# Gathering the rows of the conditional expert tiles ahead, and one last stage behind both programs

## The chip, the cores and the metric

The kernel runs on one core of one Trainium2 chip. The metric is the device time of one execution in microseconds (us), the median of several runs. A profile is one execution recorded by the hardware; its span reaches from the first instruction to the last.

## What is computed

The reference is two layers on an image of 256 channels and 48 x 48 pixels, that is 2304 tokens of 256 numbers:

```
x = x + conv_attention(group_norm(x))          # 9216 x 9216 scores, softmax without a maximum
t = tokens(x)
t = t + slice_attention(layer_norm(t))
t = t + ffn(layer_norm(t))                     # 8 experts, each token goes to 2 of them
x = image(t)
# ffn, for every token: the two largest of 8 gate values, softmax over the two, then
#   out += weight * (gelu(t @ W1[e] + b1[e]) @ W2[e] + b2[e])      for its two experts e
```

## The kernel before

The whole kernel is one function, `layers`, which the program holds twice. The first program computes the attention sums without subtracting a maximum. While it runs it notes the largest and smallest of these sums, and makes a verdict of one number, `bad`. The wrapper `tile_conv_attn_hybrid_kernel` loads `bad` into a register of every engine (L1170) and enters a second program under a branch (`tc.If(again > 0)`, L1173), which does everything again with maxima. With these inputs `bad` is 0 and the second program is jumped over.

The change touches the expert stage and what follows it. The router has put the 4608 (token, expert) pairs into tiles of 128 rows, each of one expert. At least `SURE` = 36 tiles are always used; up to `NSL` = 43 can be. `slot_t` holds the token numbers of each tile, `slot_w` the weights, `expert_i` each tile's expert, and `used_i` how many tiles are used. For a tile s:

- `load(s)` (L1030) gathers the 128 token rows from the DRAM tensor `tn_d` into a buffer `xs`, by an indirect DMA that GpSimd (POOL) issues (L1033), and loads the expert's first matrix, 1 MB, into `w1` by a DMA of SyncE (SP, L1040). Both have rings of two buffers.
- `turn` transposes the rows on TensorE (PE): two matmuls `pt`, copied by VectorE (DVE) to `xT`.
- `first` does 32 matmuls `ph` (first matrix) and eight Gelu activations on ScalarE (ACT).
- `second` does 16 matmuls `py` (second matrix, which lies in SBUF for all experts). After six of them it calls `meanwhile`, which turns the rows of a coming tile. Then DVE adds the bias and multiplies by the weight into `y`, and POOL adds the 128 rows of `y` to the DRAM tensor `t_d` with an indirect DMA (L1090). Each such addition waits for the one before it to land.

The sure tiles run in a plain loop with two tiles in flight: `first(s)`, the loads of tile s+2, then `second(s-1)`. The tiles from 36 on stand in nested branches (L1132 to L1136), since their number is known only at run time:

```
for s in range(SURE, NSL):
    more.enter_context(tc.If(used > s))
    if s + 1 < NSL:
        loaded[s + 1] = load(s + 1)
    second(s, first(s, *turned.pop(s)), lambda: turn_next(s + 1))
```

So inside the body of tile s the rows of tile s+1 are gathered, and `second(s)` turns them. Three of these bodies are entered in the profiled execution: tiles 36, 37 and 38.

The last stage stands at the end of `layers`: five DMAs of SP read `t_d` into tiles `tt`, PE transposes them (L1155), DVE and ACT copy them to `ob` (L1159, L1161), and SP writes five blocks of the output. Each of the two programs has its own copy of this stage.

Order: calls through `pe`, `dve`, `act`, `pool` and `sp` are pinned to the order of the program on their engine (the helper at L57, which is why most rows of the profile bear L57). Calls through `nc.gpsimd` and `nc.sync`, such as the gathers, the additions to `t_d` and the `w1` loads, are placed by the framework's scheduler, which also inserts all semaphores. The content of a branch is placed as a unit. Where a branch is not entered, every engine passes a short block that raises its semaphores to what the skipped code would have left; on POOL this block holds one INC_SWDGE_SEM for the semaphores of the DMAs that POOL issues.

Of the kernel before, what the change touches and what calls it, by code (L numbers as in the profile page):

```python
# [9 lines left out]
FP = mybir.dt.float32  # L10
# [5 lines left out]
P = 128  # L16
C = 256
NT = 2304
# [18 lines left out]
NSL = (2 * NT - E) // P + E  # L37
SURE = 2 * NT // P
# [24 lines left out]
def layers(  # L63
    ctx: ExitStack,
    tc: tile.TileContext,
    bad,
    x, Wq, bq, Wk, bk, Wv, bv, Wo, bo,
    W0, b0, Ws, bs, Wqkv, bqkv, Wout, bout,
    Wg, bg, W1, b1, W2, b2,
    out,  # L70
):

    nc = tc.nc
    x_v = x[0].rearrange("(c p) h w -> p c (h w)", p=P)
    out_v = out[0].rearrange("(c p) h w -> p c (h w)", p=P)

    const = ctx.enter_context(tc.tile_pool(name="const", bufs=1))
    pe, dve, act, pool, sp = (  # L80
        InOrder(tc, e) for e in (nc.tensor, nc.vector, nc.scalar, nc.gpsimd, nc.sync)
    )
    small = ctx.enter_context(tc.tile_pool(name="small", bufs=2))


    ident = const.tile([P, P], FP, name="ident")
    make_identity(nc, ident)
    ones = const.tile([P, P], FP, name="ones")
    nc.vector.memset(ones, 1.0)

# [3 lines left out]
        out=gmat, in_=gmat, pattern=[[-8, 16], [0, 8]], compare_op=ALU.is_ge,  # L94
# [3 lines left out]
        out=gmat, in_=gmat, pattern=[[8, 16], [0, 8]], compare_op=ALU.is_ge,  # L98
# [24 lines left out]
    )  # L123
    dram = ctx.enter_context(tc.tile_pool(name="dram", bufs=1, space=bass.MemoryType.DRAM))
    tn_d = dram.tile([NT + P, C], FP, name="tn_d")
    t_d = dram.tile([NT + P, C], FP, name="t_d")
    empty = const.tile([P, C], FP, name="empty")
    nc.vector.memset(empty, 0.0)
    token1 = const.tile([P, NTT], FP, name="token1")
# [107 lines left out]
    with proj, tc.tile_pool(name="ps_pj", bufs=5, space=PSUM) as ps_pj, tc.tile_pool(  # L237
        name="ps_w", bufs=2, space=PSUM
# [175 lines left out]
    def turn(i, ps):  # L414

        for c in range(2):
            pe.transpose(ps[:, C + c * P : C + (c + 1) * P], tn[:, i % 6, c * P : (c + 1) * P], ident)

        def keep():
            act.copy(tnT[:, i % 3], ps[:, C : 2 * C].rearrange("p (c t) -> p c t", c=2))  # L420

        return [(4, keep)]
# [592 lines left out]
    with tc.tile_pool(name="ps_h", bufs=1, space=PSUM) as ps_h, tc.tile_pool(  # L1015
        name="ps_y", bufs=1, space=PSUM
    ) as ps_y, tc.tile_pool(name="ps_t", bufs=1, space=PSUM) as ps_t, tc.tile_pool(
        name="ps_j", bufs=1, space=PSUM
    ) as ps_j:

        def ring(pool, n, shape, name):
            return cycle([pool.tile(shape, FP, name=f"{name}{k}") for k in range(n)])

        ring_xs, ring_w1 = ring(fp, 2, [P, C], "xs"), ring(fp, 2, [P, 2, HID], "w1")
        ring_xT, ring_hid = ring(fp, 2, [P, 2, P], "xT"), ring(fp, 2, [P, NHC, P], "hid")
        ring_y = ring(fp, 2, [P, C], "y")
        ring_ph, ring_py = ring(ps_h, 3, [P, 4, P], "ph"), ring(ps_y, 2, [P, C], "py")
        ring_pt = ring(ps_t, 2, [P, 2, P], "pt")

        def load(s):  # L1030

            xs = next(ring_xs)
            nc.gpsimd.indirect_dma_start(  # L1033
                out=xs, out_offset=None, in_=tn_d[:, :],
                in_offset=bass.IndirectOffsetOnAxis(ap=slot_t[:, s : s + 1], axis=0),
                bounds_check=NT + P - 1, oob_is_err=True,
            )
            w1 = next(ring_w1)
            e = expert_of(s, mybir.EngineType.SP)
            nc.sync.dma_start(  # L1040
                out=w1, in_=W1[bass.ds(e, 1)].rearrange("e (c p) f -> p (e c) f", p=P)
            )
            return xs, w1

        def turn(xs):

            pt = next(ring_pt)
            for c in range(2):
                pe.transpose(pt[:, c, :], xs[:, c * P : (c + 1) * P], ident)
            xT = next(ring_xT)  # L1050
            dve.tensor_copy(xT, pt)
            return xT

        def first(s, xT, w1):

            e = expert_of(s, mybir.EngineType.Activation)
            hid = next(ring_hid)
            for f0 in range(0, NHC, 4):
                ph = next(ring_ph)
                for f in range(f0, f0 + 4):  # L1060
                    for c in range(2):
                        pe.matmul(
                            ph[:, f - f0, :], w1[:, c, f * P : (f + 1) * P], xT[:, c, :],
                            start=(c == 0), stop=(c == 1),
                        )
                for f in range(f0, f0 + 4):
                    act.activation(
                        hid[:, f, :], ph[:, f - f0, :], AF.Gelu, bias=b1_e[:, bass.ds(e, 1), f],
                    )
            return hid  # L1070

        def second(s, hid, meanwhile):

            e = expert_of(s, mybir.EngineType.PE)
            py = next(ring_py)
            for f in range(NHC):
                pe.matmul(
                    py, hid[:, f, :],
                    w2_sb[:, bass.ds(e, 1), f, :].rearrange("p e d -> p (e d)"),
                    start=(f == 0), stop=(f == NHC - 1),  # L1080
                )
                if f == 2:
                    meanwhile()
            e = expert_of(s, mybir.EngineType.DVE)
            y = next(ring_y)
            dve.tensor_tensor(
                y, py, b2_e[:, bass.ds(e, 1), :].rearrange("p e d -> p (e d)"), ALU.add
            )
            dve.tensor_scalar(y, y, slot_w[:, s : s + 1], None, ALU.mult)
            nc.gpsimd.indirect_dma_start(  # L1090
                out=t_d[:, :], out_offset=bass.IndirectOffsetOnAxis(ap=slot_t[:, s : s + 1], axis=0),
                in_=y, in_offset=None, bounds_check=NT + P - 1, oob_is_err=True,
                compute_op=ALU.add,
            )

        loaded = {s: load(s) for s in range(2)}
        turned, hid = {}, {}

        def turn_next(s):
            if s < NSL:  # L1100
                xs, w1 = loaded.pop(s)
                turned[s] = turn(xs), w1

        def judge():

            both = fp.tile([P, 2], FP, name="both", tag="judge")
            for k, op in enumerate((ALU.max, ALU.min)):
                dve.tensor_reduce(both[:, k : k + 1], ends_of[:, k, :], AX.X, op)
            dve.tensor_scalar(both[:, 0:1], both[:, 0:1], HIGH, None, ALU.is_gt)
            dve.tensor_scalar(both[:, 1:2], both[:, 1:2], LOW, None, ALU.is_lt)  # L1110
            dve.tensor_tensor(both[:, 0:1], both[:, 0:1], both[:, 1:2], ALU.max)
            pm = ps_j.tile([1, P], FP, name="pm")
            pe.transpose(pm, both[:, 0:1], ident)
            dve.tensor_reduce(bad, pm, AX.X, ALU.max)

        turn_next(0)
        for s in range(SURE):
            hid[s] = first(s, *turned.pop(s))
            if s + 2 <= SURE:
                loaded[s + 2] = load(s + 2)  # L1120
            if s == 0:
                turn_next(1)
            else:
                second(s - 1, hid.pop(s - 1), lambda: turn_next(s + 1))
            if s == 4 and bad is not None:
                judge()
        second(SURE - 1, hid.pop(SURE - 1), lambda: None)
        used = nc.values_load(
            used_i, min_val=0, max_val=NSL,
            skip_runtime_bounds_check_because="it is a sum of counts, cut at NSL",  # L1130
        )
        with ExitStack() as more:  # L1132
            for s in range(SURE, NSL):
                more.enter_context(tc.If(used > s))
                if s + 1 < NSL:
                    loaded[s + 1] = load(s + 1)  # L1136
                second(s, first(s, *turned.pop(s)), lambda: turn_next(s + 1))


    with tc.tile_pool(name="fin", bufs=len(TBLOCKS)) as fin, tc.tile_pool(  # L1140
        name="ps_f", bufs=4, space=PSUM
    ) as ps_f:
# [7 lines left out]
        for (t0, n), tt in zip(TBLOCKS, tts):  # L1150
# [9 lines left out]
                else:  # L1160
                    nc.scalar.copy(ob[:, c, 0:n], pt[:, 0:n])  # L1161
            sp.dma_start(out=out_v[:, :, t0 : t0 + n], in_=ob[:, :, 0:n])


@with_exitstack
def kernel(ctx: ExitStack, tc: tile.TileContext, *args):
    verdict = ctx.enter_context(tc.tile_pool(name="verdict", bufs=1))
    bad = verdict.tile([1, 1], mybir.dt.int32, name="bad")
    layers(tc, bad, *args)
    again = tc.nc.values_load(  # L1170
        bad, min_val=0, max_val=1, skip_runtime_bounds_check_because="it is the result of a comparison"
    )
    with tc.If(again > 0):  # L1173
        layers(tc, None, *args)


# [33 lines left out]
```

## Time and profile before

| | us |
|---|---|
| median of 3 runs | 1649.94 (1649.25 to 1652.01) |
| the profiled execution's own time | 1650.91 |
| its span, first to last instruction | 1649.2 |
| PE busy in the span | 1576.2 (96%) |
| DVE, ACT, POOL busy | 1046.9, 810.0, 147.1 |
| start to the end of the router, by stretch | 0 to 1324 |
| sure tiles | about 1324 to 1592 |
| conditional tiles | about 1592 to 1626 |
| last stage, jump over the second program, end | about 1626 to 1649.2 |

In the timelines each line has the start, the duration, the engine, line and operation, the tile written and those read, the count, and in square brackets how long the engine had been idle and what ended that. "PEld" is PE's weight load. A "q" behind an engine's name means its sequencer, which waits, loads registers, branches and issues DMAs without being busy. In the views of one line, the durations are the smallest, the median and the largest in ns, and then come the first and the last start in us.

### The profile page before, as it was taken

The page shows a single profiled execution, that of the slowest core. Times are in us where ns is not written, and L with a number is a line of the kernel's source. Part 1 is how long each engine was busy: PE and PEld are TensorE (multiplying, and loading weights), DVE is VectorE, ACT ScalarE, POOL GpSimd, SP SyncE. Part 2 cuts the span into 40 slices and gives each one's busy share as a digit, 9 for nine tenths or more (in the row PEclk, how much of TensorE's full clock was granted, in tenths as well). Part 3 has the DMA queues.
Part 4 walks back from the last instruction along what each step waited for, and adds up shares of the span by engine and source line. Part 5 has one row for each costly group of instructions (what it writes and reads, how often), then busy time and mean ns, then how long its engine had stood idle before and what let it go on. Part 6 is the DMA issues. An engine that isn't in the chain of part 4 may idle for free.

```text
span 1649.2 us, 31729 instructions
## 1 busy us (share of the span) xinstructions
PE 1576.2 (96%) x13178; PEld 795.1 (48%) x13178; DVE 1046.9 (63%) x1361; ACT 810.0 (49%) x1100; POOL 147.1 (9%) x126
## 2 busy tenths in 40 slices
PE   7999999999999999999999999999997589999984
PEld 3633443333333333333333333333345489999984
DVE  6577777687777786886877877868774811111111
ACT  2355555565655655655655556556551323333321
POOL 0000000000000000000000000000000323333321
PEclk9999999999999999999999999999996689999998
DMA  4000000000000000000000000000006356666655
GB/s 134 1 1 1 1 1 1 1 1 1 2 1 1 2 1 2 1 1 1 1 1 1 1 1 1 1 1 1 1 2 230 115 183 187 173 185 191 174 143 160
DMA packets 39735, 78.87 MB, mean 48 GB/s; under 512 B 3534, under 2 KB 26139, under 8 KB 39451
## 3 DMA queue, kind: packets, MB, share of 16 engines
q1 hardware_dynamic: 32042, 66.35, 11.9%
q0 software_dynamic: 7536, 10.36, 3.6%
q8 instruction: 108, 1.77, 0.5%
q14 instruction: 49, 0.39, 0.1%
HBM read 64.24 MB, written 12.45 MB: 47 GB/s over the span
## 4 chain that ended last, share of the span: by engine, by line
PE 92%; DVE 3%; DMA 2%; issue 2%; ACT 0%; POOL 0%; SPq 0%; ACTq 0%; POOLq 0%; DVEq 0%
PE s L57 33%; PE av L57 33%; PE ph L57 8%; PE py L57 8%; PE pa L57 2%; PE pb L57 1%; PE pw L57 1%; PE pp L292 1%; PE pp L296 1%; PE pp L321 1%; DMA t_d<-y,slot_t 1%; PE pt L57 1%; DMA Wq_raw<-in_L_conv_Wq_dram 0%; DVE s L57 0%; PE pm L57 0%
## 5 line engine op out<-in xcount | busy, mean ns | idle before, releaser
L57 DVE TENSOR_TENSOR acc<-acc,p 128x1024 f32<-128x1024 f32 x612 | 748.0, 1222 | 256.8 <-ACT p L57 248.6
L57 ACT ACTIVATE p<-s 128x1024 f32<-128x1024 f32 x648 | 662.7, 1023 | 493.5 <-PE s L57 483.4
L57 PE MATMUL av<-p,v_sb 64*64 64x512 f32 x5184 | 675.8, 590 | 1.4 <-ACT p L57 0.7
L57 PE MATMUL s<-q,kk 64*64 64x512 f32 x5184 | 674.9, 589 | 0.0
L57 PEld LDWEIGHTS s<-q,kk 64*64 64x64 f32 x5184 | 202.0, 133 | 351.2 <-issue 180.9
L57 PEld LDWEIGHTS av<-p,v_sb 64*64 64x64 f32 x5184 | 195.9, 131 | 358.0 <-ACT p L57 202.3
L57 ACT ACTIVATE hid<-ph,bcol 128x128 f32<-128x128 f32 x312 | 89.0, 368 | 231.2 <-PE ph L57 217.6
L57 PEld LDWEIGHTS ph<-xT,w 128*128 128x128 f32 x1248 | 148.0, 195 | 3.0 <-DVE xT L57 0.9
L57 PE MATMUL py<-w_sb,hid 128*128 x624 | 149.3, 383 | 0.0
L57 PE MATMUL ph<-xT,w 128*128 128x128 f32 x1248 | 148.3, 278 | 0.5 <-DVE xT L57 0.5
L57 POOL TENSOR_TENSOR rstd_t<-ve,mhalf 128x1 f32<-128x1 f32 (+1 forms) x21 | 27.6, 1313 | 1251.0 <-DVE ve L57 1251.0
L57 DVE COPY xT<-pt 128x256 f32<-128x256 f32 x40 | 17.0, 424 | 181.2 <-PE pt L57 181.2
L57 PEld LDWEIGHTS py<-w_sb,hid 128*128 128x128 f32 x624 | 114.2, 193 | 12.7
L1090 POOL DMA_INDIRECT t_d<-y,slot_t x39 | 61.8, 1585 | 101.5 <-DVE y L57 91.2
L57 DVE TENSOR_TENSOR y<-py,b_bc 128x256 f32<-128x256 f32 x39 | 16.5, 424 | 70.7 <-PE py L57 70.7
L1033 POOL DMA_INDIRECT xs<-tn_d,slot_t x40 | 42.6, 1066 | 105.7 <-PE pt L57 96.2
L57 DVE RECIPROCAL rinv<-pb 128x256 f32<-128x256 f32 x18 | 31.5, 1749 | 0.0
L57 PE MATMUL pt<-ident,xs 128*128 128x128 f32 x80 | 16.2, 283 | 11.8 <-DMA xs<-tn_d,slot_t 11.8
L57 DVE TENSOR_TENSOR acc<-p 128x1024 f32<-128x1024 f32 x18 | 22.1, 1225 | 8.4 <-ACT p L57 8.4
L309 DVE TENSOR_SCALAR q<-pp,bcol 64x512 f32<-64x512 f32 (+1 forms) x30 | 20.8, 694 | 8.8 <-PE pp L292 8.4
L57 PE MATMUL pw<-what,t_sb 128*128 128x86 f32 x72 | 15.7, 422 | 6.7 <-POOL what L57 6.7
L57 DVE TENSOR_REDUCE up<-av 128x512 f32<-128x1024 f32 x18 | 21.9, 1216 | 0.0
(248 smaller groups left out, 601.9 us busy)
## 6 DMA issues: line engine op xcount, KB each, us to landing
w<-in_L_ffn_W_dram SPq DMA_DIRECT2D x40, 1024.0 KB
w_sb<-in_L_ffn_W_dram SPq DMA_DIRECT2D x8, 1024.0 KB
x_sb<-in_x_dram SPq DMA_DIRECT2D x4, 576.0 KB
t_d<-t_sb SPq DMA_DIRECT2D x3, 768.0 KB
tn_d<-tn SPq DMA_DIRECT2D x3, 768.0 KB
tt<-t_d SPq DMA_DIRECT2D x4, 512.0 KB
out_dram<-ob SPq DMA_DIRECT2D x4, 512.0 KB
b_bc<-in_L_ffn_b_dram SPq DMA_DIRECT2D x1, 1024.0 KB
```

Of the source, the lines that this page charges most:

```text
L57: return self.tc.keep_in_program_order(getattr(self.engine, name)(*args, **kwargs))
L292: nc.tensor.matmul(pq[:, 0:tn], WqT[:, c, cols], xn[:, c, toks], start=(c == 0), stop=(c == 1))
L296: nc.tensor.matmul(pk[:, 0:tn], WkT[:, c, cols], xn[:, c, toks], start=(c == 0), stop=(c == 1))
L309: nc.vector.tensor_scalar(dst, pq[rows, 0:tn], bcol[rows, B_Q + m : B_Q + m + 1], 0.125, ALU.add, ALU.mult,)
L321: nc.tensor.matmul(pv[:, 0:C], xn[:, c, i * P : (i + 1) * P], WvT[:, c, :], start=(c == 0), stop=(c == 1),)
L1033: nc.gpsimd.indirect_dma_start(out=xs, out_offset=None, in_=tn_d[:, :], in_offset=bass.IndirectOffsetOnAxis(ap=slot_t[:, s : s + 1], axis= ...
L1090: nc.gpsimd.indirect_dma_start(out=t_d[:, :], out_offset=bass.IndirectOffsetOnAxis(ap=slot_t[:, s : s + 1], axis=0), in_=y, in_offset=None ...
```

## The change

The gathers of the tiles 36 to 42 are moved out of the branches into the loop of the sure tiles, with a buffer of their own for each (seven tiles `late_xs` of 128 x 256). They are written into the iterations s = 17 to 23. `load` is split into `rows` (gather) and `load_w1`. The `w1` loads stay where they are. In all, 43 gathers are then issued where the profiled execution issued 40.

The last stage is taken out of `layers` and put behind the branch of the second program, where both programs share it; `t_d` and the identity `ident`, which it uses, are made by the wrapper. So the register load of `bad` and the jump over the second program now stand ahead of the last stage; before, they stood behind it.

```diff
@@ layers, expert stage
+        late_xs = iter([fp.tile([P, C], FP, name=f"late_xs{s}") for s in range(SURE, NSL)])
-        def load(s):
-            xs = next(ring_xs)
+        def rows(s, xs):
             nc.gpsimd.indirect_dma_start(out=xs, ...)
+            return xs
+
+        def load_w1(s):
             w1 = next(ring_w1)
...
-        loaded = {s: load(s) for s in range(2)}
+        for s in range(2):
+            xs[s], w1[s] = rows(s, next(ring_xs)), load_w1(s)
...
         for s in range(SURE):
-            hid[s] = first(s, *turned.pop(s))
+            hid[s] = first(s, xT.pop(s), w1.pop(s))
+            if s + 2 < SURE:
+                xs[s + 2] = rows(s + 2, next(ring_xs))
             if s + 2 <= SURE:
-                loaded[s + 2] = load(s + 2)
+                w1[s + 2] = load_w1(s + 2)
+            ahead = s + 1 - SURE // 2
+            if 0 <= ahead < NSL - SURE:
+                xs[SURE + ahead] = rows(SURE + ahead, next(late_xs))
...
                 more.enter_context(tc.If(used > s))
                 if s + 1 < NSL:
-                    loaded[s + 1] = load(s + 1)
-                second(s, first(s, *turned.pop(s)), lambda: turn_next(s + 1))
+                    w1[s + 1] = load_w1(s + 1)
+                second(s, first(s, xT.pop(s), w1.pop(s)), lambda: turn_next(s + 1))
@@ wrapper
+    make_identity(nc, ident)
+    t_d = dram.tile([NT + P, C], FP, name="t_d")
-    layers(tc, bad, *args)
+    layers(tc, bad, ident, t_d, *args[:-1])
     again = nc.values_load(bad, ...)
     with tc.If(again > 0):
-        layers(tc, None, *args)
+        layers(tc, None, ident, t_d, *args[:-1])
+    sp = InOrder(tc, nc.sync)
+    with tc.tile_pool(name="fin", ...) as fin, ...:     # the last stage, moved here as it was
...
```

More of the change, by code (lines that the diff above doesn't have):

```diff
@@ L65, in layers @@
     tc: tile.TileContext,
-    bad,
+    bad, ident, t_d,
     x, Wq, bq, Wk, bk, Wv, bv, Wo, bo,
@@ L69, in layers @@
     Wg, bg, W1, b1, W2, b2,
-    out,
 ):
@@ L76, in layers @@
     x_v = x[0].rearrange("(c p) h w -> p c (h w)", p=P)
-    out_v = out[0].rearrange("(c p) h w -> p c (h w)", p=P)
     const = ctx.enter_context(tc.tile_pool(name="const", bufs=1))
-    pe, dve, act, pool, sp = (
-        InOrder(tc, e) for e in (nc.tensor, nc.vector, nc.scalar, nc.gpsimd, nc.sync)
-    )
+    pe, dve, act, pool = (InOrder(tc, e) for e in (nc.tensor, nc.vector, nc.scalar, nc.gpsimd))
     small = ctx.enter_context(tc.tile_pool(name="small", bufs=2))
-    ident = const.tile([P, P], FP, name="ident")
-    make_identity(nc, ident)
     ones = const.tile([P, P], FP, name="ones")
@@ L125, in layers @@
     tn_d = dram.tile([NT + P, C], FP, name="tn_d")
-    t_d = dram.tile([NT + P, C], FP, name="t_d")
     empty = const.tile([P, C], FP, name="empty")
@@ L1042, in load @@
             )
-            return xs, w1
+            return w1
         def turn(xs):
@@ L1094, in second @@
             )
-        loaded = {s: load(s) for s in range(2)}
-        turned, hid = {}, {}
+        xs, w1, xT, hid = {}, {}, {}, {}
+        for s in range(2):
+            xs[s], w1[s] = rows(s, next(ring_xs)), load_w1(s)
         def turn_next(s):
             if s < NSL:
-                xs, w1 = loaded.pop(s)
-                turned[s] = turn(xs), w1
+                xT[s] = turn(xs.pop(s))
         def judge():
@@ L1135, in layers, with kernel @@
                 if s + 1 < NSL:
-                    loaded[s + 1] = load(s + 1)
-                second(s, first(s, *turned.pop(s)), lambda: turn_next(s + 1))
+                    w1[s + 1] = load_w1(s + 1)
+                second(s, first(s, xT.pop(s), w1.pop(s)), lambda: turn_next(s + 1))
+@with_exitstack
+def kernel(ctx: ExitStack, tc: tile.TileContext, *args):
+    nc = tc.nc
+    out_v = args[-1][0].rearrange("(c p) h w -> p c (h w)", p=P)
+    both = ctx.enter_context(tc.tile_pool(name="both", bufs=1))
+    bad = both.tile([1, 1], mybir.dt.int32, name="bad")
+    ident = both.tile([P, P], FP, name="ident")
+    make_identity(nc, ident)
+    dram = ctx.enter_context(tc.tile_pool(name="t", bufs=1, space=bass.MemoryType.DRAM))
+    t_d = dram.tile([NT + P, C], FP, name="t_d")
+    layers(tc, bad, ident, t_d, *args[:-1])
+    again = nc.values_load(
+        bad, min_val=0, max_val=1, skip_runtime_bounds_check_because="it is the result of a comparison"
+    )
+    with tc.If(again > 0):
+        layers(tc, None, ident, t_d, *args[:-1])
+    sp = InOrder(tc, nc.sync)
     with tc.tile_pool(name="fin", bufs=len(TBLOCKS)) as fin, tc.tile_pool(
@@ L1162, in layers @@
             sp.dma_start(out=out_v[:, :, t0 : t0 + n], in_=ob[:, :, 0:n])
[L1165 to L1168, printed above, removed]
-    layers(tc, bad, *args)
[L1170 to L1173, printed above, removed]
-        layers(tc, None, *args)
 _INS = [
```

## The prediction

> **What bounds the kernel now.** I read the page first: PE is busy 96% of the span and carries 92% of the chain that ended last. A change that doesn't touch PE's work can gain only where PE stands idle, so I looked for idle PE in the two stretches that the change touches. The windows by stage give 263.8 us of PE work in the 268 us of the sure tiles, 25.6 in the 34 us of the conditional tiles, and 5.9 in the last 24 us. The timeline of PE from 1587 us on shows the holes:
>
> ```profile
> 1592.57 3.73 PE L57 MATMUL ph<-xT,w 128*128 128x128 f32 x32
> 1596.14 1.46 PE L57 MATMUL py<-w_sb,hid 128*128 x6
> 1601.87 0.69 PE L57 MATMUL pt<-ident,xs 128*128 128x128 f32 x2 [4.27 <-DMA xs<-tn_d,slot_t]
> 1602.35 4.47 PE L57 MATMUL py<-w_sb,hid 128*128 x10
> 1606.62 3.91 PE L57 MATMUL ph<-xT,w 128*128 128x128 f32 x32
> 1610.36 1.46 PE L57 MATMUL py<-w_sb,hid 128*128 x6
> 1614.21 0.44 PE L57 MATMUL pt<-ident,xs 128*128 128x128 f32 x2 [2.39 <-DMA xs<-tn_d,slot_t]
> ...
> 1622.66 0.44 PE L57 MATMUL pt<-ident,xs 128*128 128x128 f32 x2 [0.98 <-DMA xs<-tn_d,slot_t]
> 1622.93 2.32 PE L57 MATMUL py<-w_sb,hid 128*128 x10
> 1634.55 4.36 PE L1155 MATMUL pt<-ident,tt 128*128 128x128 f32 x24 [9.29 <-DMA tt<-t_d]
> ```
>
> In each conditional body the transposes of the next rows wait for the gather, and the ten `py` behind the longest wait take 4.47 us, where the same ten take 2.32 in the third body. The timeline of POOL says why the gather is late: it is issued in the body, right behind the addition of the tile before.
>
> ```profile
> 1594.89 1.55 POOL L1090 DMA_INDIRECT t_d<-y,slot_t  x1 [2.94 <-PE ph L57]
> 1596.75 1.10 POOL L1033 DMA_INDIRECT xs<-tn_d,slot_t  x1 [0.30 <-issue]
> 1607.96 1.58 POOL L1090 DMA_INDIRECT t_d<-y,slot_t  x1 [10.11 <-DVE y L57]
> ...
> 1626.39 1.58 POOL L1090 DMA_INDIRECT t_d<-y,slot_t  x1 [5.46 <-DVEq L1132]
> ```
>
> Behind the last addition comes the last stage. The chain that ended last has this addition's landing, the first `tt` load and the transposes in a row. Meanwhile POOL goes to the end of the branches (L1132), loads `bad` (L1170), and jumps over the second program (L1173). The views of these lines give its steps:
>
> ```profile
> 1626.39 3.84 DMA t_d<-y,slot_t
> 1630.38 4.04 DMA tt<-t_d
> ...
> L1132 POOLq INC_SWDGE_SEM  x1: 1775/1775/1775, 1626.9 to 1626.9; - x1
> ...
> L1170 POOLq TENSOR_LOAD <-bad x1: 311/311/311, 1628.9 to 1628.9; - x1
> ...
> L1173 POOLq EVENT_SEMAPHORE  x6: 17/30/43, 1632.0 to 1632.4; - x6
> L1173 POOLq COMPARE_BRANCH  x1: 55/55/55, 1629.3 to 1629.3; - x1
> L1173 POOLq INC_SWDGE_SEM  x1: 1746/1746/1746, 1632.5 to 1632.5; - x1
> L1173 PEldq COMPARE_BRANCH  x1: 4167/4167/4167, 1641.1 to 1641.1; - x1
> ```
>
> The reader is to see two things here: POOL is through with the jump only at 1634.3, 7.9 us behind the issue of its last addition; and nobody waits for that now, for the `tt` loads start at 1630.4.
>
> **The change part by part.**
>
> *Gathers out of the branches: minus 10.8 us.* In the sure loop a tile costs PE 3.57 (`ph`) + 1.30 (six `py`) + 0.22 (`pt`) + 2.16 (ten `py`) = 7.25 us, start to start; POOL's additions repeat at just that distance. Three bodies at this pace end at 1592.57 + 21.75 = 1614.3. They end now at about 1625.1 (1622.93 + 2.16). So 10.8 us: 7.6 of it is the waiting itself, the rest the matmuls that ran slower behind the waits. Is something else late once the rows are there? The `w1` of tile 38 is issued at 1596.3, when the `ph` of tile 36 are done, and lands at 1601.5 by the DMA record; at the new pace it is needed at 1607.1. Gelu: the last of the eight ends 1.4 us behind the last `ph` (the timeline of ACT), and its `py` starts over 3 us behind it. Each addition waits for the last one's landing, 3.8 us, within a period of 7.25. So none of these is due. If only the pure waits went, it would be 7.6.
>
> *Gathers in the sure loop: 0.* Seven come in at s = 17 to 23, and tile 36's leaves the place where it was; in all there are three more. One occupies POOL for 1.06 us. POOL's two instructions of an iteration take 1.06 + 1.59 of 7.25 us, so the third has room; an addition that is delayed by 1.1 us has nobody waiting for it before the next, 7.25 us on, and `xs` of the coming tile lands about 9 us before its `pt`. On the DMA side 128 KB is an eighth of the 1 MB `w1` of the same period, whose transfer takes 5.5 of the 10.9 us that it has. If this cover were gone, one iteration would pay up to 1.1 us. The gathers go through `nc.gpsimd`, so the scheduler may bring them forward to the start of the loop, where `w1` of tile 2 lands at 1340.2 and is needed at 1342.4: 2.2 us of room. Seven gathers of 128 KB beside it are nearly as much as that matrix. I bound this by 0 and 2 and take 0. Less than 0 is excluded: the loop has no wait that they could remove.
>
> *Last stage behind the jump: plus 4.0 us.* It reads `t_d`, which the skipped program would have written as well, so I expect the first `tt` load to wait until POOL has raised its DMA semaphores in the skip block of L1173. POOL's path from the last addition is the one above: 0.5 to the first INC_SWDGE_SEM, 1.8 for it, 0.2, 0.3 for the register, 2.7 from the branch to the first instruction behind it, 0.5 for semaphores, 1.75 for the second INC_SWDGE_SEM: 7.9 us. The `tt` loads now start 4.0 us behind the addition (1630.4 - 1626.4) and would then start 7.9 to 8.0 behind it: plus 4.0. The other engines' jumps are shorter from there: PE's branch out of the bodies took 3.3 us and its far jump 4.2, but it starts 3 us before the addition and would be through at about 5.8 us behind it; it then waits for `tt` anyway until 12. DVE, the slowest behind its branch (1641.5 to 1646.0), would be through at about 5. SP leaves the bodies 15 us before the addition. If the fetch on POOL took DVE's 4.5 instead of 2.7, as five engines now jump within 2 us, it would be 5.7; if `tt` didn't wait for POOL's skip block, 0.
>
> [...] POOL's row, 55 ns for the branch and 2.7 us until the next instruction, [...] so I take 2.7. [...] the jump is moved from beside the output DMAs onto the path.
>
> *The end: minus 1.3 us.* Now SP issues the last output block (done at 1642.0), loads `bad`, and jumps; its first semaphore behind the jump is at 1646.9 and the span ends at 1649.2. The output has landed at 1646.6. Without a jump SP needs only what is left of its list of waits (0.06 us each, twelve of them) and the closing barrier of 0.85: 1647.5 to 1648.1. So 1.1 to 1.7 less; I take 1.3.
>
> *The wrapper's identity and `t_d`, other places in SBUF:* 0. The same two or three instructions at the head of POOL's queue, beside the load of `x`; bounds plus and minus 1 for a shifted schedule in the first 1324 us, as nothing in the page prices it.
>
> Sum: -10.8 + 4.0 - 1.3 = -8.1 us. The profiled execution took 1650.91, 1.7 more than its span and 1.0 more than the median; it would take 1642.8. Against the median of 1649.94 that is 1641.8.
>
> **The rivals.**
>
> *The last stage doesn't wait for POOL's jump.* Then -12.1: 1637.8. For it: all landings are known by 1630.2. Against it: a wait set at compile time must hold for both ways through the branch. 0.10.
>
> *The jump or the gathers cost more.* Fetch of 4.5 on POOL (+1.8), up to 2 us at `w1` of tile 2: 1643.6 to 1646. For it: five jumps at once, freely placed gathers. 0.16.
>
> *The rows are there, but another wait takes the gather's place* (a body's start, `w1`, the addition), and only about half of 10.8 is gained: 5.4 - 4.0 + 1.3 = 2.7 less, 1647.2, which is no difference. Against it: the room worked out above. 0.05.
>
> *Slower: the scheduler puts the late gathers ahead of the first one.* Place: POOL's queue at 1324.5, where PE waits 4.2 us for tile 0's rows. The first two gathers there start 1.64 us apart, so seven cost 11.5 us on PE's path: 1641.8 + 11.5 = 1653.3. It decides from five on (8.2). Against it: they are ready no earlier than tile 0's, and later in the program; the gathers of before all came in the program's order. 0.04.
>
> **How the numbers follow.** My forecast has 0.65, by itself 1639.5 to 1644.5. From 1637.5 to 1646 the range takes in the first rival and nearly all of the second, and leaves out some 0.13 (the last two and the edges). A measurement here tells apart about 0.2%, 3.3 us. Faster: 0.65 + 0.10 + 0.16 = 0.91; same 0.05; slower 0.04.
>
> **What would show it.** Right: no idle time of PE before `pt<-ident,xs` from 1592 on; bodies 7.25 us apart; ten `py` in 2.3 us throughout; the last addition at about 1615.6; INC_SWDGE_SEM of the far jump ending 7.9 us behind it and the first `tt` load directly after; last output DMA to the end of the span about 1.3 shorter than the 7.2 us of now. Wrong: `tt` loads 4 us behind the last addition (first rival), a hole in PE near 1342 (second), or the first `pt<-ident,xs` several us later than 1327.7 (slower).

## The result: 0.55% faster, as forecast, with the last term of the sum mis-sized

Four runs of each kernel gave 1641.41 us (1639.91 to 1642.84) for the changed kernel and 1650.41 (1649.25 to 1652.01) for the kernel before: a ratio of 0.9945, 95% interval 0.9927 to 0.9962. The forecast was 1641.8. The profiled execution of the changed kernel took 1642.84 and has a span of 1641.1; the one of before had 1649.2.

PE's timeline after the change, the lines that answer to the holes shown before:

```profile
1593.44 3.73 PE L57 MATMUL ph<-xT,w 128*128 128x128 f32 x32
1597.01 1.46 PE L57 MATMUL py<-w_sb,hid 128*128 x6
1598.31 0.38 PE L57 MATMUL pt<-ident,late_xs 128*128 128x128 f32 x2
1598.53 2.32 PE L57 MATMUL py<-w_sb,hid 128*128 x10
1600.69 3.73 PE L57 MATMUL ph<-xT,w 128*128 128x128 f32 x32
...
1607.94 3.73 PE L57 MATMUL ph<-xT,w 128*128 128x128 f32 x32
...
1613.02 2.32 PE L57 MATMUL py<-w_sb,hid 128*128 x10
1628.75 5.90 PE L1175 MATMUL pt<-ident,tt 128*128 128x128 f32 x36 [13.40 <-DMA tt<-t_d]
```

No line of the three bodies has an idle time in brackets any more, the `ph` start 7.25 us apart (1593.44, 1600.69, 1607.94), and the ten `py` take 2.32 throughout. The one hole left is larger than before: 13.40 us in front of the last stage instead of 9.29.

The last addition in POOL's timeline:

```profile
1616.47 1.56 POOL L1086 DMA_INDIRECT t_d<-y,slot_t  x1 [5.49 <-DVEq L1133]
```

POOL's INC_SWDGE_SEM in the view of the end of the bodies (L1133), and its lines and PE's in the view of the far jump (L1155):

```profile
L1133 POOLq INC_SWDGE_SEM  x1: 1101/1101/1101, 1616.9 to 1616.9; - x1
```

```profile
L1155 POOLq EVENT_SEMAPHORE  x6: 17/30/43, 1622.0 to 1622.5; - x6
...
L1155 PEldq COMPARE_BRANCH  x1: 4381/4381/4381, 1617.6 to 1617.6; - x1
L1155 POOLq COMPARE_BRANCH  x1: 55/55/55, 1618.6 to 1618.6; - x1
L1155 POOLq INC_SWDGE_SEM  x1: 1092/1092/1092, 1622.6 to 1622.6; - x1
```

SP's timeline before the change, and then after it:

```profile
1630.38 2.95 SPq L57 DMA_DIRECT2D tt<-t_d  x5
1637.26 4.77 SPq L57 DMA_DIRECT2D out_dram<-ob  x5
```

```profile
1624.27 2.98 SPq L57 DMA_DIRECT2D tt<-t_d  x5
1631.46 4.71 SPq L57 DMA_DIRECT2D out_dram<-ob  x5
```

Read in this order: the last addition at 1616.47; POOL leaves the bodies, branches at 1618.6, and has its first instruction behind the jump only at 1622.0; its second INC_SWDGE_SEM ends at 1623.7; the first `tt` load follows at 1624.27. So the loads now stand behind the jump, 7.8 us from the addition instead of 4.0, and 4.9 us lie from the end of the last output issue (1631.46 + 4.71) to the end of the span instead of 7.2.

The same execution cut into five parts, the way the later runs are compared. "First pt" is the start of the first transposes of tile 0; "landed" is the last record of the DMA that carries the last output block.

| one profiled execution | first pt | to the last addition | to the first tt load | to the end of the last output issue | to landed / to the end |
|---|---|---|---|---|---|
| before | 1327.65 | 298.74 | 3.99 | 11.65 | 4.61 / 7.16 |
| changed | 1328.51 | 287.96 | 7.79 | 11.90 | 3.25 / 4.92 |
| difference | +0.86 | -10.78 | +3.80 | +0.25 | / -2.24 |

The differences sum to -8.1, which is 1641.1 - 1649.2. That this is also the forecast's sum is in part luck: the end gained 0.9 us more than forecast, and +0.86 and +0.25 that were not in the sum took about as much back.

### The profile page after: what moved, and what is told of

Read it like the earlier page. It is cut to its first block, busy times and chain, and to the rows that moved or that the text cites. A ratio compares the mean times of both kernels' runs of the same rounds, so it can differ in the third digit from the quotient of the medians.

```text
span 1641.1 us, 31749 instructions
## 1 busy us (share of the span) xinstructions
PE 1574.2 (96%) x13178; PEld 793.9 (48%) x13178; DVE 1046.9 (64%) x1361; ACT 811.1 (49%) x1100; POOL 149.7 (9%) x129
## 4 chain that ended last, share of the span: by engine, by line
PE 93%; DVE 3%; DMA 3%; ACT 0%; issue 0%; POOL 0%; SPq 0%; ACTq 0%; POOLq 0%; DVEq 0%
PE s L57 34%; PE av L57 34%; PE ph L57 8%; PE py L57 8%; PE pa L57 2%; DMA t_d<-y,slot_t 2%; PE pb L57 1%; PE pw L57 1%; PE pp L285 1%; PE pp L289 1%; PE pp L314 1%; PE pt L57 1%; DVE s L57 0%; DMA Wq_raw<-in_L_conv_Wq_dram 0%; PE pm L57 0%; ACT p L57 0%
## 5 line engine op out<-in xcount | busy, mean ns | idle before, releaser
L1026 POOL DMA_INDIRECT xs<-tn_d,slot_t x36 | 38.3, 1064 | 93.0 <-PE pt L57 83.9
L285 PE MATMUL pp<-t_sb,WqT 128*128 128x512 f32 (+1 forms) x40 | 19.0, 601 | 0.3 <-DVE t_sb L276 0.3
```

What stands on the lines that cost most here:

```text
L285: nc.tensor.matmul(pq[:, 0:tn], WqT[:, c, cols], xn[:, c, toks], start=(c == 0), stop=(c == 1))
L1026: nc.gpsimd.indirect_dma_start(out=xs, out_offset=None, in_=tn_d[:, :], in_offset=bass.IndirectOffsetOnAxis(ap=slot_t[:, s : s + 1], axis= ...
```

## Experiments

All versions are written from the kernel before or from the changed one. The table has the same parts of each profiled execution, and the median of each with its ratio to the kernel before in the same session (whose medians were 1651.49 for e1 to e4, 1650.79 for e5 to e8, and 1650.65 for e9 and e10). The ratio comes from all runs and is not exactly that of the medians.

| version | first pt | to last addition | to tt | to last output issue | landed / end | median | ratio, interval |
|---|---|---|---|---|---|---|---|
| e1 gathers ahead only | 1326.23 | 287.78 | 3.89 | 11.72 | 4.67 / 7.53 | 1639.77 | 0.9935 (0.9921 to 0.9948) |
| e2 shared stage only | 1327.99 | 298.61 | 8.92 | 12.20 | 3.12 / 4.45 | 1652.60 | 1.0007 (0.9998 to 1.0015) |
| e3 pinned | 1327.97 | 287.92 | 7.26 | 11.83 | 3.13 / 4.80 | 1641.45 | 0.9939 (0.9924 to 0.9955) |
| e4 late gathers first | 1336.99 | 288.46 | 7.13 | 12.10 | 3.16 / 4.83 | 1650.63 | 0.9996 (0.9988 to 1.0005) |
| e5 short jump | 1327.65 | 287.90 | 4.00 | 11.85 | 3.54 / 4.87 | 1637.65 | 0.9921 (0.9906 to 0.9936) |
| e6 other tensor | 1328.34 | 287.74 | 5.29 | 12.64 | 3.02 / 4.69 | 1640.01 | 0.9934 (0.9919 to 0.9950) |
| e7 no second program | 1327.73 | 287.92 | 4.10 | 11.78 | 3.65 / 4.99 | 1636.85 | 0.9916 (0.9900 to 0.9931) |
| e8 two ahead | 1327.56 | 288.04 | 4.11 | 11.78 | 4.82 / 7.06 | 1640.27 | 0.9937 (0.9924 to 0.9951) |
| e9 spaced | 1327.38 | 287.96 | 7.59 | 11.76 | 3.22 / 4.56 | 1640.13 | 0.9935 (0.9919 to 0.9950) |
| e10 output by ACT | 1326.49 | 287.68 | 3.92 | 12.03 | 4.72 / 7.25 | 1639.45 | 0.9936 (0.9923 to 0.9950) |

### e1 and e2: each half of the change alone

```diff
e1, from the kernel before:
+ late_xs, rows(s, xs), load_w1(s) and their calls as in the change; the last stage stays at the end of layers
e2, from the changed kernel:
-            ahead = s + 1 - SURE // 2
-            if 0 <= ahead < NSL - SURE:
-                xs[SURE + ahead] = rows(SURE + ahead, next(late_xs))
                 if s + 1 < NSL:
+                    xs[s + 1] = rows(s + 1, next(ring_xs))
                     w1[s + 1] = load_w1(s + 1)
```

> Gathers ahead alone; each program keeps its own last stage in front of the jump. My account: the conditional bodies run 7.25 us apart without a wait of PE (10.8 us less than before), the first tt load starts about 4 us behind the issue of the last addition, and the end is as before (about 7.1 us from the last output DMA to the end of the span). So about 10.8 us under the kernel before, 1.9 us under the changed kernel. Rival (the shared last stage brings a gain of its own, and the gathers less): 6 to 8 us under the kernel before, so slower than the changed kernel.

> Shared last stage alone; the gathers stay in the conditional bodies. My account: PE waits for the rows in each body as before (7.6 us in three waits), the first tt load starts 7.8 us behind the last addition instead of 4.0, and the end is about 2.2 us shorter than before: about 1.8 us more than before. Rival (the shared stage brings a gain): at least 1 us less than before.

The gathers alone give the whole gain and more: 287.78 us to the last addition, 3.89 to the `tt` load, a median 11.7 us under the kernel before. The shared stage alone gains nothing (a ratio of 1.0007 whose interval includes 1). Its timeline of PE shows the old waits and the new tail:

```profile
1602.16 0.69 PE L57 MATMUL pt<-ident,xs 128*128 128x128 f32 x2 [4.25 <-DMA xs<-tn_d,slot_t]
1602.64 4.47 PE L57 MATMUL py<-w_sb,hid 128*128 x10
...
1623.14 2.32 PE L57 MATMUL py<-w_sb,hid 128*128 x10
1640.18 6.37 PE L1170 MATMUL pt<-ident,tt 128*128 128x128 f32 x36 [14.71 <-DMA tt<-t_d]
```

By the parts, its tail from the last addition to the end is 8.92 + 12.20 + 4.45 = 25.57 us against 22.80 before: 2.8 more, where I expected 1.8; the medians are 1.1 apart. Of the rival, that the shared stage brings a gain of its own, nothing is left. The medians of e1 and of the changed kernel differ by 1.6 us in the direction of this account, but their intervals overlap; the parts carry the reading (23.14 us of tail in e1, 24.61 in the changed kernel).

### e5, e6, e7: what the tail waits for

```diff
e5, from the changed kernel (the second program is left out):
+    zero = both.tile([P, C], FP, name="zero")
+    nc.vector.memset(zero, 0.0)
...
     with tc.If(again > 0):
-        layers(tc, None, ident, t_d, *args[:-1])
+        nc.gpsimd.dma_start(out=t_d[0:P, :], in_=zero)
e6, from the changed kernel (the second program writes another tensor):
+    t_2 = dram.tile([NT + P, C], FP, name="t_2")
...
     with tc.If(again > 0):
-        layers(tc, None, ident, t_d, *args[:-1])
+        layers(tc, None, ident, t_2, *args[:-1])
e7, from e1 (no second program):
-    again = tc.nc.values_load(bad, ...)
-    with tc.If(again > 0):
-        layers(tc, None, *args)
```

> The changed kernel with the second program left out: under its branch stands one DMA of POOL that writes t_d instead, so the jump is as before in its place, but short. My account (of the 7.8 us from the last addition to the first tt load, 3.5 are the code of a far target being fetched): the load starts 4.3 to 5 us behind the addition, about 3 us under the changed kernel. Rival (the semaphore work of the skip block and waits on other engines set it): 7 us or more, the time of the changed kernel within 1 us.

> The changed kernel, with a DRAM tensor of its own for the second program instead of t_d, which the last stage then doesn't read; with these inputs the second program isn't entered. My account in the prediction (tt waits for POOL's skip block because the skipped program writes t_d): POOL drops out, PE's skip block would be the last, and the tt loads start 5.5 to 6 us behind the last addition instead of 7.3 to 7.8. Rival (the tiles of the last stage lie in SBUF where both programs have had buffers, and that alone makes SP wait for POOL's block): no change, 7.3 to 7.8.

> Gathers ahead, the last stage where it was, and no second program, no load of bad and no jump at all. It prices what the jump costs at the end, and is the floor for the tail. My account: the tt loads start 3.9 us behind the last addition, the output lands 3.2 us behind its last DMA instead of 4.7, and the span ends about 4.7 us behind it instead of 7.5: 2.8 us under the version with the gathers ahead alone. Rival (the closing barrier needs its 7 us with or without a jump): within 1 us of that version.

e5 leaves the jump in its place and makes it short; with the second program the lists of semaphores in the skip blocks get shorter as well. The lines of its branch, and then its SP timeline:

```profile
L1157 POOLq COMPARE_BRANCH  x1: 55/55/55, 1617.6 to 1617.6; - x1
L1157 POOLq INC_SWDGE_SEM  x1: 1050/1050/1050, 1617.8 to 1617.8; - x1
```

```profile
1619.54 2.97 SPq L57 DMA_DIRECT2D tt<-t_d  x5
```

POOL's next instruction is 0.2 us behind the branch instead of 3.5, PE's branch takes 0.23 us instead of 4.4, and the `tt` loads start 4.0 us behind the addition (1615.55), so as early as its landing (1619.3) lets them. POOL is through 3.3 us behind the addition, before this has landed, where the changed kernel needed 7.2. Of these 3.9 us, 3.3 are the time from the branch to the next instruction, and 0.5 are six semaphores that e5's skip block doesn't have. So the far target, the code behind the whole second program, is most of the cost of the shared stage, and the branch itself, 55 ns in both, is nothing.

e6 shows which wait passes the jump on. With a tensor of its own for the second program, SP no longer waits for POOL's skip block, though that block still ends only at 1622.8. The view of its branch, and then SP's timeline:

```profile
L1156 PEldq COMPARE_BRANCH  x1: 3981/3981/3981, 1617.1 to 1617.1; - x1
L1156 POOLq COMPARE_BRANCH  x1: 55/55/55, 1618.2 to 1618.2; - x1
L1156 POOLq INC_SWDGE_SEM  x1: 1092/1092/1092, 1621.7 to 1621.7; - x1
```

```profile
1621.37 3.57 SPq L57 DMA_DIRECT2D tt<-t_d  x5
```

The loads start 5.3 us behind the addition (1616.08), a little earlier than the 5.5 to 6 expected. So it is `t_d` that ties the last stage to POOL's jump, as the prediction had it, and the reuse of SBUF doesn't (the rival). But PE's block isn't quite what comes next: the addition itself lands 4.87 us behind its issue by the DMA records, SP waits for that until 1621.0, and then 0.15 us for PE. e6 is no version to use: its last stage would not see what the second program writes.

e7 is the floor: no jump anywhere. It ends 4.99 us behind the last output issue, 2.5 less than e1. Its tail is 2.3 us shorter by the parts. The medians differ by 2.9 (2.8 expected), but they come from two sessions; each against the kernel before of its own session, e7 gains 2.2 more. e5 equals e7 within 1 us.

### e8: the same gain with the gathers left in the branches

```diff
e8, from the kernel before, with load split as in the change:
-        ring_xs = ring(fp, 2, [P, C], "xs")
+        ring_xs = ring(fp, 3, [P, C], "xs")
...
+            if s + 2 <= SURE + 1:
+                xs[s + 2] = rows(s + 2, next(ring_xs))
...
             for s in range(SURE, NSL):
                 more.enter_context(tc.If(used > s))
+                if s + 2 < NSL:
+                    xs[s + 2] = rows(s + 2, next(ring_xs))
                 if s + 1 < NSL:
                     w1[s + 1] = load_w1(s + 1)
```

> The kernel before with the gathers left in the conditional bodies, but each one tile earlier: a ring of three xs buffers, and the body of tile s gathers the rows of s+2. My account (only the lateness of the gather matters, not its place in a branch): no wait of PE in the bodies, about 10.8 us under the kernel before. Rival (a gather in a body stays behind the addition on POOL's queue and costs there): waits of 1 us or more are left in the bodies, 5 to 9 us under the kernel before.

```profile
1594.68 1.55 POOL L1091 DMA_INDIRECT t_d<-y,slot_t  x1 [2.92 <-PE ph L57]
1596.54 1.10 POOL L1031 DMA_INDIRECT xs<-tn_d,slot_t  x1 [0.30 <-issue]
```

```profile
1597.24 0.38 PE L57 MATMUL pt<-ident,xs 128*128 128x128 f32 x2
1597.46 2.32 PE L57 MATMUL py<-w_sb,hid 128*128 x10
```

These are the timelines of POOL and of PE. The gather still stands right behind the addition, at 1596.54, but it now fetches the rows of the tile after next, and the transposes at 1597.24 find theirs landed. It is 288.04 us to the last addition, as with the gathers ahead. So the branch did not cost anything by itself; the gather was one tile too late. One more buffer does here what seven do.

### e3, e9, e4: where the late gathers stand

```diff
e3, from the changed kernel: the late gathers through the pinned POOL handle (rows gets the queue as a third argument)
-                xs[SURE + ahead] = rows(SURE + ahead, next(late_xs))
+                xs[SURE + ahead] = rows(SURE + ahead, next(late_xs), pool)
e9, from the changed kernel: a dependence on DVE in the same iteration
+                late = next(late_xs)
+                dve.memset(late[:, 0:1], 0.0)
+                xs[SURE + ahead] = rows(SURE + ahead, late)
e4, from the changed kernel: all seven in front, all pinned
+        for s in range(SURE, NSL):
+            xs[s] = rows(s, next(late_xs), pool)
         for s in range(2):
-            xs[s], w1[s] = rows(s, next(ring_xs)), load_w1(s)
+            xs[s], w1[s] = rows(s, next(ring_xs), pool), load_w1(s)
...
-            ahead = s + 1 - SURE // 2
-            if 0 <= ahead < NSL - SURE:
-                xs[SURE + ahead] = rows(SURE + ahead, next(late_xs))
```

> The changed kernel, with the seven late gathers pinned to the order of the program, so that they are issued in the iterations 17 to 23 of the sure loop; in the changed kernel the scheduler has put them between the first gathers, at 1328 to 1338 us. My account (a gather among the sure tiles has room wherever it stands): the time of the changed kernel within 1 us, no wait of PE for rows or w1 in the sure loop. Rival (their early place costs something at tile 1 or 2, or shifts the start by the 0.9 us by which the first transposes came later): 1 to 2 us less than the changed kernel.

> The changed kernel, where each late gather also depends on a one-column memset by VectorE in its iteration, so that the seven are really issued one by one in the iterations 17 to 23 (pinning the gathers to the order of the program had left them at 1328 to 1337 us). My account (a gather has room wherever it stands in the sure loop): no wait of PE for rows or w1 in the sure loop, the last addition 288 us behind the first transposes as in the changed kernel, the time within 1 us of it. Rival (beside w1 and the additions a gather costs its 1.1 us each): the distance grows by 3 to 8 us.

> The slower rival of the prediction, built: the seven late gathers are issued ahead of the gather of tile 0. The changed kernel issues them 1.31 us apart. If they lie on PE's path, the first transposes come 7 x 1.31 = 9.2 us later and the time is about 9 us above the changed kernel, so 0 to 1 us above the kernel before. The prediction priced them at 1.64 us each: 11.5 us later, about 3 us above the kernel before. If the DMA engines catch up with the gathers (the rows of tile 0 land sooner behind their issue), less than 9.

The changed kernel issues the late gathers far earlier than the iterations in which they are written. Its POOL timeline:

```profile
1325.27 1.34 POOL L1026 DMA_INDIRECT xs<-tn_d,slot_t  x1 [8.22 <-DVE slot_w L57]
1326.91 1.02 POOL L1026 DMA_INDIRECT xs<-tn_d,slot_t  x1 [0.30 <-issue]
1328.23 1.01 POOL L1026 DMA_INDIRECT late_xs<-tn_d,slot_t  x1 [0.30 <-issue]
1329.54 1.01 POOL L1026 DMA_INDIRECT late_xs<-tn_d,slot_t  x1 [0.30 <-issue]
```

e3 left them there (1327.7 to 1336.9), so it is a second run of the changed kernel and answers nothing on their place; its median is 1641.45. e9 moves them:

```profile
L57 DVE MEMSET late_xs<- x7: 59/59/59, 1452.1 to 1495.6; 128x1 f32 x7
L1026 POOL DMA_INDIRECT late_xs<-tn_d,slot_t x7: 1054/1058/1066, 1454.3 to 1497.9; - x7
```

They go out one per tile, and PE has no wait in the sure loop; it is 287.96 us to the last addition, exactly as in the changed kernel. A gather has room at either place.

e4 is the slower rival, built: seven gathers ahead of tile 0's rows. Its PE timeline:

```profile
1336.99 0.69 PE L57 MATMUL pt<-ident,xs 128*128 128x128 f32 x2 [13.44 <-DMA xs<-tn_d,slot_t]
```

The wait for tile 0's rows grows from 4.31 to 13.44 us, 9.1 more, for seven issues 1.31 us apart (9.2). The median is 9.2 us above the changed kernel, and not to be told from the kernel before (0.9996, an interval that includes 1). So the mechanism is real, at 1.31 us for each of the seven; the order of the first gathers decides over the whole gain.

### e10: the output DMAs from another queue

```diff
e10, from e1:
-            sp.dma_start(out=out_v[:, :, t0 : t0 + n], in_=ob[:, :, 0:n])
+            nc.scalar.dma_start(out=out_v[:, :, t0 : t0 + n], in_=ob[:, :, 0:n])
```

> Gathers ahead, last stage in front of the jump, and the five output DMAs issued by ACT instead of SP, so that SP is through with its jump before the output lands. My account of the end (SP's register load, its jump of 4.1 us and its list of semaphores stand behind the last output DMA, and the fetches lie beside the landing): from the last output DMA to the end of the span 6 to 6.5 us instead of 7.5, the time about 1 us under the version with the gathers ahead alone. Rival (ACT's own jump takes SP's place, or ACT waits for DVE's half of a block and delays its copies): within 0.5 us of that version, or above it.

A miss: 7.25 us at the end instead of 7.53, and the median within 0.3 us of e1. SP is behind its jump early now (its first semaphore there at 1627.7, 6.3 us behind its branch), but it doesn't get through its list of semaphores: it stands still there until the output lands, at 1634.2 to 1634.8, and then has 2.5 us of semaphores and the barrier left. ACT's jump lasts until 1634.5, so the rival, ACT in SP's place, describes it about as well; the two are not told apart.

### A version under both kernels

e1, the gathers ahead and a last stage for each program, is a complete kernel and leaves out the half of the change that costs: 1639.77 us. e10 is the same within its scatter, and e8 reaches 1640.27 with one more buffer. Against the kernel before all three are 0.6% faster; against the changed kernel their advantage of 1 to 2 us is inside the intervals. e5 and e7 leave the second program out and only show how much is left: 2 to 3 us.

## Why the prediction was right, step by step

**Gathers, -10.8: right.** -10.78 in the profile, and -11.0 in e1. The argument that nothing else would be due (`w1`, Gelu, landings of additions) holds: bodies of 7.25 us. e8 adds what the prediction didn't separate: the lateness is that of one tile, not of the branch.

The prediction counted 7.6 us of waits and gave the other 3.2 to matmuls that ran slower behind them, without a reason. The view of the kernel before by stretches has one. Behind the five pairs of busy time and count stands the clock that PE was granted:

```profile
1595.00:1605.00 10.00, 5.73 (x27) 4.70 (x26) 0.42 (x1) 1.90 (x7) 2.54 (x2) 0.76 0.43 131
1605.00:1615.00 10.00, 7.61 (x48) 6.70 (x47) 1.09 (x3) 2.28 (x8) 2.68 (x2) 0.90 0.42 126
1615.00:1625.00 10.00, 9.02 (x59) 7.96 (x57) 1.32 (x4) 2.28 (x8) 2.68 (x2) 1.00 0.18 36
```

In narrower stretches it is 0.50 from 1600.1, inside the wait of 4.27 us, to 1606.9, and 1.00 in the rest of the bodies, the waits of 2.39 and 0.98 us included. PE works for 5.0 us of that stretch, so the half clock is some 2.5 of the 3.2 us (an estimate from these two numbers). In the bodies of the changed kernel, of e1 and of e8 the clock is 1.00; in e2, where the waits are back, it is 0.50 from 1600.4 to 1607.2. So the gathers ahead gain the clock as well as the waits.

**Gathers in the sure loop, 0: right, at another place than written.** The prediction allowed for the scheduler bringing them forward with up to 2 us at tile 2's `w1`. It brought them forward, five between the gathers of tiles 1 and 2, and PE has no hole there (the `ph` of tile 2 start at 1343.27, right behind the `py`).

**Last stage behind the jump, +4.0: right in sum (+3.80), by terms that cancelled.** e6 shows the wait that was forecast. But the two INC_SWDGE_SEM were put in at 1.78 and 1.75 and took 1.10 and 1.09, 1.3 us less. The wait behind POOL's branch was put in at 2.7 and took 3.5, 0.8 more and within the range of 2.7 to 4.5 that was given; the four other versions with the shared stage, both programs and the gathers ahead have 2.8 to 3.3. And SP needs 0.6 us more than reckoned for its list of ten waits behind POOL's block. That the sum came out is luck. (The seven steps of the list add up to 7.75, not 7.9; the views of before give 7.9.) Where the gathers stay in the branches as they were (e2), INC_SWDGE_SEM takes 1.75 again and the loads start 8.9 us behind the addition. Why it takes 1.75 in the kernel before and e2 and 1.05 to 1.10 in all the others stays open.

**The price of the far jump.** POOL's 2.7 us was read from one row of the kernel before, without a run that separates the branch from the wait behind it. e5 separates them: the same branch to a near target costs 0.2 us instead of 3.5 on POOL, 0.23 instead of 4.4 on PE. In the changed kernel 23 of the 25 branches at L1133 take 34 to 93 ns (the other two are PE's, 196 and 3606 ns), and the rows of the far jump itself are as short on four engines: 55 ns on POOL, 60 on ACT, 69 on DVE, 50 on SP. There the wait isn't in the branch's own row; it has to be read from the start of the next instruction, 3.4, 2.6, 3.0 and 4.6 us behind that row. On PE it is in the row (4381 ns). That these waits are for code being fetched is a reading of the DMA records, which have packets of the kind `instruction`: in the 3.6 us behind the last addition 6 of them start in the changed kernel, where DVE, PE and POOL jump, and 2 in the kernel before, where PE and DVE jump some 15 us later.

**The end, -1.3: the sign right, the size wrong, -2.24.** The failing term is "the output has landed at 1646.6", which was kept as it was. The landing came 1.36 us earlier behind the last issue (3.25 instead of 4.61). What stands behind the landing shrank by 0.88 (1.67 instead of 2.55), less than the 1.1 to 1.7 reckoned: seven of the twelve waits of SP's list still came behind the landing, and the closing barrier took 1.2 us instead of 0.85. The output lands 4.6 us behind its last issue where the engines make the far jump beside it (before, e1, e8, e10: 4.6 to 4.8) and 3.0 to 3.7 where they don't (all others). So the jump not only stood in SP's queue, it also held up the output itself; e1 and e7, which differ by the second program and its jump alone, have 4.67 and 3.65.

**Not in the sum:** +0.86 ahead of the first transposes and +0.25 in the last stage. The start of the first transposes lies between 1327.4 and 1328.5 in the versions with the shared stage but e4, and between 1326.2 and 1327.7 in the others. Part of that is scatter: e1 and e10, the two earliest, had the granted clock at half for 3.4 us near 1243, where all others had it for 6.8. Whether something of the +0.86 is the wrapper's identity and `t_d` stays open; the prediction allowed 1 us for them.

**Chances:** the first rival (no wait for POOL's jump) is what e6 builds and is wrong for this kernel; the second (a dearer fetch) was true on POOL in part, 0.8 of its 1.8 us, and covered by the cheaper INC_SWDGE_SEM (1.09 instead of 1.75); the slower rival's mechanism comes true in e4's order. Its price per gather was read from the first pair, 1.64 us, where one is 1.31: all seven, not five, are needed to eat the gain, and they make the kernel no slower than before.

## What to carry to other kernels

The gathers inside the run-time branches cost what they were late, not that they were in a branch: issued one tile earlier in e8, they left 288.04 us to the last addition, against 287.96 with the gathers ahead and 298.74 before. So ask for which tile a gather is issued, and one more buffer may do. The jump over the second program cost 2.6 us (ACT) to 4.6 us (SP) in the changed kernel, and 6.3 for SP in e10. Where a landing lay beside it, it was cheaper but not free: at the end of e1 it cost 2.5 us against e7. Don't let the common path's next stage depend on a semaphore that the skipped code would have raised: its loads started 7.79 us behind the last addition in the changed kernel, and 5.29 in e6, where they didn't wait for POOL's skip block. When two codes are to share a stage, look first at what the skipped one writes.

## What the runs showed of the hardware that was not expected

DMAs that ran beside the fetches of code landed later here. The last addition to `t_d` lands 4.6 to 5.3 us behind its issue in the changed kernel, e3, e4, e6 and e9, where the far jumps of DVE, PE and POOL start within 2.1 us behind it, and 3.6 to 4.0 in all others. e2 is among these, at 3.75, in spite of its jump. The DMA records have packets of the kind `instruction`, read here as the code that is fetched, and their number goes with it: in the 3.6 us behind the addition's issue 6 of them start in each of the five late versions, 2 or 3 in the versions without those jumps, and 4 in e2, where PE and POOL jump 0.5 to 0.9 us later. In the same way 6 or 7 start between the issue and the landing of the last output block where it lands 1.0 to 1.8 us later, and 0 or 1 in all others. In bytes and time it is little. The changed kernel's last 29 us have, in packets, MB and share of the DMA engines:

```profile
q8 instruction: 4, 0.07, 1.1%
q14 instruction: 10, 0.08, 1.0%
```

That is 14 packets, but q8's are 16 KB each and took 1.0 to 2.0 us by the DMA records, and a transfer is counted as landed here with its last record. That its last piece stood behind a code packet was not shown directly; the difference with and without the jump was.
